# Two fused transformer layers on one core: the first weight pairs' sums moved into the preamble, and block 1's rotary scores moved behind two projection steps

## The chip, the cores and the metric

The kernel runs on one core of a Trainium2 chip. The metric is device time in microseconds of one execution, the median of several runs. Names of engines: TensorE (PE) does matmuls and writes PSUM; VectorE (DVE) and ScalarE (ACT) work element by element on SBUF and PSUM; GpSimd (POOL) works on SBUF; SP issues most of the DMA transfers.

## The reference, cut to what matters

Four batches of 256 tokens, 256 features, go through two layers with a layer norm after each half:

```python
x = layernorm(x + L0_attn(x));  x = layernorm(x + L0_ffn(x))
x = layernorm(x + L1_attn(x));  x = layernorm(x + L1_ffn(x))

# L0_attn: 16 heads, plain part 128 wide, rotary part 64 wide
q_rope, k_rope = apply_rope(q_rope, cos, sin), apply_rope(k_rope, cos, sin)
scores = einsum('bqhd,bkhd->bhqk', q_nope, k_nope) / sqrt(128) \
       + einsum('bqhd,bkhd->bhqk', q_rope, k_rope) / sqrt(64)
out = einsum('bhqk,bkhd->bqhd', softmax(scores), v) @ Wo.T
```

`L0_ffn` is a gated network with a Walsh-Hadamard transform of its hidden row, `L1_attn` an mLSTM block with a gated network of its own, `L1_ffn` a gated network with int8 weights. All arithmetic is float32.

## The kernel before

**Attention.** The 16 heads make eight pairs (`NPAIR`), the tokens two halves of 512 (two batches each). A *block* h is one pair p = h // 2 and one half n = h % 2, so there are 16 blocks. Each block's scores, softmax and weighted values (`fast_block`) run together with the projections of the next block (`fast_projections(h + 1)`), whose matmuls fill TensorE while the softmax runs on the other engines. Block 0's own projections are made plainly, in a preamble (`projections(0)`).

**Seven products for eight.** From block 1 on, a projection is a 2 x 2 product of blocks (two column halves of the weights c, two batches b, two halves of the features i), made with seven block products instead of eight. They need sums and differences of the inputs (`input_sums(n)`: four instructions, kept in `xsum`) and of the weights (`weight_sums(p)`, kept in `wsums[p % 2]`: four combinations, each as one instruction for the three plain groups q, k, v, 384 columns, and one for the rotary group, 128 columns: eight in all). `weight_sums(0)` stands in the preamble, `weight_sums(1)` in front of block 1, `weight_sums(p)` in front of block 2p - 2 for the others. Each stands behind the last projection step of the block before, by `behind(...)`, which orders an instruction behind another of its own engine and adds no wait between engines.

**Steps.** The projection products are cut into steps A1 to A7 (groups "rotary" and "q", in the PSUM banks `mm`) and B1 to B7 (groups "k" and "v", in the banks `sc`, or `ot` while block 0 runs). A step is two to four matmuls (on the chip each is two passes) and the copies (ScalarE) or additions (VectorE) that take its results out. Lists fix the order of the steps: `EARLY[0]` and `EARLY[1]` for blocks 0 and 1, `ORDER` for the others; V and O are the weighted values and the output product of the block before. `EARLY[1]` begins `A1 A2 B1 B2 A6 A7 B6 B7`. A7 accumulates on a bank whose content A2's additions (`qn`, line 375) must first have read.

**Rotary part.** When A3 and A4 are done, `turn(0)` and `turn(1)` swap neighbouring rows (a shuffle on VectorE, line 291) and multiply and add on GpSimd, three instructions each (lines 294 to 296); the last writes `kr`. In `projections(0)` the same is done at lines 183 to 188. `turned_weights` copies the rotary columns of a pair into another order on GpSimd (line 115).

**Scores.** `scores` issues 16 matmul passes per score bank group for the plain part (line 434), then those of the rotary part (line 445), which need `kr`. A score bank is one of two `sc` or two `pt` banks; it is read by `maxima` (line 456, VectorE) and by two exponentials (line 465, ScalarE).

**Order of loads.** SP's queue takes the loads in program order: pair 0's weights in pieces, the tables, the second half of `xT`, `w_o` of pair 0, the residual rows `acc` (two loads of 0.5 MB, line 136), pair 1's weights (1 MB) and `w_o`, then three 1-MB weights of the first feed-forward network. All of `acc` is first used when the output product of block 0 is added to it (line 547).

**Later stages.** `ffn0(n)`, `mlstm(n)`, `ffn1(n)` are generators; each `yield` carries an amount of time. `merge(first, other)` runs `first` and, for every amount it yields, takes steps of `other` until their amounts (1.7 for most) cover it, so that `other`'s matmuls fill TensorE while `first` waits for the other engines. `mlstm_in` yields 9.0 after a norm, in front of the transposes of its result `hin`; `chain(take(1, one), [6.0])` runs the norm at the start of `ffn1(0)` and covers it with 6.0 of ffn0(1). A scheduler then fixes the order on each engine.

Of the kernel before, what the change touches and what calls it, by code (L numbers as in the profile page):

```python
# [39 lines left out]
def tile_two_layers(ctx: ExitStack, tc: tile.TileContext, a: dict, out: bass.AP):  # L40
# [90 lines left out]
    had = cst[:, 512:640]  # L131
    mask = cst[:, 640:768]
    ident = cst[:, 896:1024]
    acc = [wts.tile([P, NJH, D], F32, tag=f"acc{n}", name=f"acc{n}") for n in range(2)]
    for n in range(2):
        nc.sync.dma_start(acc[n], a["x"][:, n * NJH : (n + 1) * NJH, :])
    weights[1], w_os[1] = load_pair(1), load_output(1)

    def ff_weight(name, engine=nc.sync, dtype=F32):

# [15 lines left out]
    rotated = {}  # L156
    QB, XB = P // 32, S // 32

    nothing = lambda: None

    def projections(h):


        p, n = divmod(h, 2)
        w, wr = weights[p]
        qn = attn.tile([P, 2, HALF], F32, tag="qn", name="qn")
        kn = attn.tile([P, 2, HALF], F32, tag="kn", name="kn")
        qr = attn.tile([P, HALF], F32, tag="qr", name="qr")
        kr = attn.tile([P, HALF], F32, tag="kr", name="kr")
        v = attn.tile([P, NJH, 2 * P], F32, tag="v", name="v", bufs=3)  # L170

        def product(wcols):
            ps = bank("mm")
            mm_k(ps, wcols, lambda i: xT[:, i, n * HALF : (n + 1) * HALF], KC)
            return ps

        def rope(k, scale, dst):

            ps = product(lambda i: wr[:, i, k, :])
            raw = attn.tile([P, HALF], F32, tag="raw", name="rope_raw", bufs=3)  # L180
            nc.scalar.mul(raw, ps, scale)
            swp = attn.tile([P, HALF], F32, tag="swp", name="rope_swp", bufs=3)
            nc.vector.stream_shuffle(swp, raw, SWAP)
            by_b = lambda t: t.rearrange("p (b s) -> p b s", s=S)
            cs, sn = (t.unsqueeze(1).to_broadcast([P, 2, S]) for t in (cos, sin))
            nc.gpsimd.tensor_tensor(by_b(raw), by_b(raw), cs, ALU.mult)
            nc.gpsimd.tensor_tensor(by_b(swp), by_b(swp), sn, ALU.mult)
            rotated[h] = nc.gpsimd.tensor_tensor(dst, raw, swp, ALU.add)

        def nope_q2():  # L190

            ps = [bank("mm") for _ in range(2)]
            for i in range(KC):
                for e in range(2):
                    nc.tensor.matmul(
                        ps[e], lhsT=w[:, i, e * P : (e + 1) * P], rhs=xT[:, i, n * HALF : (n + 1) * HALF],
                        start=(i == 0), stop=(i == KC - 1),
                    )
            for e in range(2):
                nc.scalar.mul(qn[:, e, :], ps[e], QSCALE)  # L200

        def nope_q(e):
            ps = product(lambda i: w[:, i, e * P : (e + 1) * P])
            return nc.scalar.mul(qn[:, e, :], ps, QSCALE)

        def nope_k(e):
            ps = product(lambda i: w[:, i, 384 + e * P : 384 + (e + 1) * P])
            return nc.scalar.copy(kn[:, e, :], ps)

        def values(jj):  # L210
            ps = bank("mm")
            for t in range(2):
                j = n * NJH + 2 * jj + t
                mm_k(
                    ps[:, t * 256 : (t + 1) * 256],
                    lambda i: xT[:, i, j * P : (j + 1) * P],
                    lambda i: w[:, i, 768:1024],
                    KC,
                )
            return nc.vector.tensor_copy(  # L220
                v[:, 2 * jj : 2 * jj + 2, :], ps.rearrange("p (t d) -> p t d", t=2)
            )

        units = [lambda: rope(0, RSCALE, qr), lambda: rope(1, 1.0, kr)]
        units += [lambda e=e: nope_q(e) for e in range(2)] if h else [nope_q2, nothing]
        units += [lambda e=e: nope_k(e) for e in range(2)]
        units += [lambda jj=jj: values(jj) for jj in range(2)]
        return (qn, kn, qr, kr, v), units
# [22 lines left out]
        nc.vector.tensor_tensor(three, xT[:, 1, tok(1)], xT[:, 0, tok(1)], ALU.subtract)  # L251
        return nc.vector.tensor_tensor(four, xT[:, 1, tok(0)], two, ALU.subtract)

    def weight_sums(p):

        w, wr = weights[p]
        sums = wsums[p % 2]
        plain = lambda i, c: w[:, i, :].rearrange("p (g c x) -> p g c x", g=3, c=3)[:, :, c, :]
        rot = lambda i, c: wr[:, i, c, :]
        for at, three in (  # L260
            (lambda m: sums[:, m, 0:384].rearrange("p (g x) -> p g x", g=3), plain),
            (lambda m: sums[:, m, 384:512], rot),
        ):
            nc.vector.tensor_tensor(at(0), three(0, 1), three(1, 1), ALU.add)
            nc.vector.tensor_tensor(at(1), at(0), three(0, 0), ALU.subtract)
            nc.vector.tensor_tensor(at(2), three(0, 0), three(0, 1), ALU.subtract)
            last = nc.vector.tensor_tensor(at(3), three(1, 0), at(1), ALU.subtract)
        return last

    def fast_projections(h):  # L270
# [16 lines left out]
        def turn(c):  # L287

            swp = attn.tile([P, HALF], F32, tag="swp", name="rope_swp", bufs=3)
            with tc.issue_after(settled["softmax"].ins):  # L290
                nc.vector.stream_shuffle(swp, raw[c], SWAP)  # L291
            by_b = lambda t: t.rearrange("p (b s) -> p b s", s=S)
            cs, sn = (t.unsqueeze(1).to_broadcast([P, 2, S]) for t in (cos, sin))
            nc.gpsimd.tensor_tensor(by_b(raw[c]), by_b(raw[c]), cs, ALU.mult)  # L294
            nc.gpsimd.tensor_tensor(by_b(swp), by_b(swp), sn, ALU.mult)  # L295
            rotated[h] = nc.gpsimd.tensor_tensor((qr, kr)[c], raw[c], swp, ALU.add)
# [121 lines left out]
        steps.update({"B" + k: f for k, f in pair_of_groups("sc" if h > 1 else "ot", (1, 2)).items()})  # L418
        return (qn, kn, qr, kr, v), steps

    def scores(t, batches):

# [5 lines left out]
        for bb in batches:  # L430
            for e in range(2):
                for qt in range(2):
                    in_turn(
                        lambda: nc.tensor.matmul(  # L434
                            ps[bb][e][:, qt * S : (qt + 1) * S],
                            lhsT=qn[:, e, queries(bb, qt)], rhs=kn[:, e, keys(bb)],
                            start=(qt == 0), stop=False, skip_group_check=True,
                        )
                    )
        for bb in batches:  # L440
            for qt in range(2):
                for e in range(2):
                    rows = slice(e * DR, (e + 1) * DR)
                    in_turn(
                        lambda: nc.tensor.matmul(  # L445
                            ps[bb][e][:, qt * S : (qt + 1) * S],
                            lhsT=qr[rows, queries(bb, qt)], rhs=kr[rows, keys(bb)],
                            start=False, stop=(qt == 1), skip_group_check=True,
                        )
                    )  # L450
# [98 lines left out]
        steps = halves()  # L549
        return lambda: next(steps, None)  # L550

    settled = {}
    behind = lambda ins: tc.issue_after(ins.ins)

    ORDER = "A1 A2 V00 A6 V01 A7 A5 B1 B2 A3 A4 B6 B7 V10 B5 V11 O0 B3 O0 B4 O1 O1".split()
    EARLY = {
        0: "A1 A2 B1 A6 B2 A7 A5 B6 A3 B7 B5 A4 B3 B4".split(),
# [1 line left out]
    }  # L559
    def fast_block(h, t, probs, prev, steps):  # L560

        ps = scores(t, (0, 1))
        crossed = crossing()
        po, outs, last = {}, {}, {}
        top = [maxima(ps[bb][e]) for bb in range(2) for e in range(2)]
        found = [exponentials(ps[0][0], top[0])]

# [5 lines left out]
        for step in EARLY.get(h, ORDER):  # L573
# [6 lines left out]
                    outs[bb] = output_product(h - 1, bb, po[bb])  # L580
            elif step[0] == "O":
                settled["block"] = outs[int(step[1])]()
            else:
                settled["block"] = last[step] = steps[step]()
            if step == "A1":
                with behind(last["A1"]):
                    found.append(exponentials(ps[0][1], top[1]))
# [17 lines left out]
    tiles, units = projections(0)  # L605
    settled["inputs"] = input_sums(0)
    with behind(settled["inputs"]):
        for u in units[2:4] + units[0:2]:
            u()
        settled["weights"] = weight_sums(0)  # L610
    for u in units[4:6]:
        u()
    with behind(settled["weights"]):
        for u in units[6:]:
            settled["values"] = u()
    with behind(settled["values"]):
        input_sums(1)
    with behind(rotated[0]):
        turned_weights(*weights[1])
    after_it, steps = fast_projections(1)  # L620
    probs, prev = None, None
    for h in range(NB - 1):
        for p in range(1, NPAIR):
            if h == max(1, 2 * p - 2):
                with behind(settled["block"]):
                    weight_sums(p)
        probs = fast_block(h, tiles, probs, prev, steps)
        if h % 2 == 0:
            if 0 < h < NB - 2:
# [220 lines left out]
    def mlstm_in(n, t):  # L850

        hin = work.tile([P, NJH, D], F32, tag="hin", name=f"hin{n}")
        rmsnorm(xb[n], hin)
        yield 9.0
        fm = feature_major(n)
        transposed(hin, fm, "m", vecs[:, 0:2])
        yield 1.7
# [371 lines left out]
    def chain(*streams):  # L1229
        for s in streams:  # L1230
            yield from s
# [10 lines left out]
    run(one)  # L1242
    merge(mlstm(0), other)
    one = ffn1(0, "d")
    merge(chain(take(1, one), [6.0]), other)
    run(take(1, one))
    run(other)
    q_gate, q_up, q_down = (ff_weight(k, nc.gpsimd, F32R) for k in ("q_gate", "q_up", "q_down"))
# [123 lines left out]
```

## Time and profile before

| | us |
|---|---|
| median of three runs | 699.29 (698.92 to 705.53) |
| the profiled execution | 699.31 |
| its span, first to last instruction | 697.5 |
| mean granted TensorE clock | 0.995 |
| DMA moved | 45.43 MB, mean 65 GB/s |
| PE busy, 0 to 20 us of the span | 19.22 |
| PE busy, 20 to 40 | 19.59 |
| PE busy, 40 to 60 | 17.41 |
| PE busy, 60 to 80 and 80 to 100 | 20.00 each |
| PE busy, 640 to 697 | 49.95 of 57 |

Durations and starts are those of one profiled execution. A matmul of float32 appears as two passes, and matmuls overlap, so the time that one costs is the distance from start to start. A line of the waits reads: engine, its line, what it waited for, microseconds in all, how often, the longest. A line of the timeline reads: start, length, engine, line of the kernel, operation, what is written and read, shapes, number of instructions merged into the line, and, in brackets, idle time just before it and what ended it.

### The profile page before, as it was taken

The numbers are of one execution on the slowest core, as the hardware profiler recorded it, in microseconds if no ns is written. First come the engines' busy times: TensorE is split into PE (matmuls) and PEld (weight loads), VectorE is DVE, ScalarE is ACT, GpSimd is POOL, SyncE is SP. The second block draws the span as 40 slices with busy tenths as digits, with TensorE's granted clock in tenths as the row PEclk, the third lists the DMA queues.
The fourth block names the chain that finished last, engine by engine and source line by source line (L and its number), as shares of the span: only waits on it lengthen the run. The fifth ranks groups of instructions, "written<-read, shape, count | busy, mean of one in ns | idle before, by whom it ended". The sixth has DMA issues, their size and how long they took to land.

```text
span 697.5 us, 9871 instructions
## 1 busy us (share of the span) xinstructions
PE 685.2 (98%) x3408; PEld 533.0 (76%) x3408; DVE 455.4 (65%) x1238; ACT 260.5 (37%) x773; POOL 178.4 (26%) x187
## 2 busy tenths in 40 slices
PE   9989999999999999999999999999999999999995
PEld 5878888988988898898888764745685558648885
DVE  3996766676577478467547664373878468844767
ACT  2432542443354254334425331037312561111652
POOL 4254314413632740751243100004000130000210
PEclk9999999999999999999999999999999999999999
DMA  8543143232332421521431442003030300000001
GB/s 261 222 122 60 30 109 61 46 95 57 61 97 40 103 65 31 137 56 20 122 62 32 151 96 37 0 1 122 1 121 0 123 2 1 0 0 1 1 0 61
DMA packets 49026, 45.43 MB, mean 65 GB/s; under 512 B 9520, under 2 KB 42704, under 8 KB 47824
## 3 DMA queue, kind: packets, MB, share of 16 engines
q1 hardware_dynamic: 48112, 41.00, 22.8%
q0 software_dynamic: 432, 3.15, 1.3%
q10 hardware_dynamic: 432, 0.66, 0.3%
q8 instruction: 27, 0.44, 0.3%
q14 instruction: 23, 0.19, 0.1%
HBM read 25.61 MB, written 1.08 MB: 38 GB/s over the span
## 4 chain that ended last, share of the span: by engine, by line
PE 89%; DVE 6%; DMA 1%; POOL 1%; ACT 1%; issue 1%; SPq 0%; DVEq 0%; ACTq 0%
PE ps_mm L350 13%; PE ps_d L70 11%; PE ps_m L70 8%; PE ps_ot L70 8%; PE ps_mm L70 8%; PE ps_sc L342 6%; PE ps_sc L350 6%; PE ps_d L797 6%; PE ps_d L1110 4%; PE ps_sc L434 3%; PE ps_pt L434 3%; PE ps_sc L445 2%; PE ps_m L1029 2%; PE ps_m L797 2%; PE ps_pt L445 2%; PE ps_m L766 1%
## 5 line engine op out<-in xcount | busy, mean ns | idle before, releaser
L294 POOL TENSOR_TENSOR rope_raw<-rope_raw,cst 128x512 f32<-128x512 f32 x30 | 38.5, 1285 | 187.3 <-DVE rope_swp L291 187.3
L465 ACT ACTIVATE pr<-ps_sc,nmax 128x256 f32<-128x256 f32 x64 | 29.8, 476 | 128.0 <-DVE nmax L456 128.0
L70 PE MATMUL ps_mm<-w_o,oT 128*128 128x256 f32 x256 | 62.2, 379 | 0.0
L70 PE MATMUL ps_ot<-prT,v 128*128 128x256 f32 x240 | 61.3, 380 | 0.2 <-issue 0.2
L70 PE MATMUL ps_d<-fm,w 128*128 128x512 f32 x128 | 56.8, 595 | 0.0
L547 DVE TENSOR_TENSOR acc<-ps_mm,acc 128x512 f32<-128x512 f32 x32 | 22.1, 691 | 49.8 <-PE ps_mm L70 49.6
L70 PEld LDWEIGHTS ps_mm<-w_o,oT 128*128 128x128 f32 x256 | 46.7, 190 | 5.3
L988 POOL TENSOR_TENSOR ex<-cst,ex 128x512 f32<-128x512 f32 x16 | 19.7, 1263 | 111.9 <-DMA ex<-far 111.9
L70 PEld LDWEIGHTS ps_ot<-prT,v 128*128 128x128 f32 x240 | 43.3, 190 | 5.6 <-issue 0.9
L70 PEld LDWEIGHTS ps_d<-fm,w 128*128 128x128 f32 x128 | 23.9, 190 | 27.2 <-issue 25.4
L350 PE MATMUL ps_mm<-xsum,wsum 128*128 128x256 f32 x180 | 43.9, 380 | 0.4 <-DVE qn L375 0.4
L456 DVE TENSOR_REDUCE nmax<-ps_sc 128x2 f32<-128x512 f32 x32 | 20.6, 686 | 35.7 <-PE ps_sc L445 35.7
L483 DVE STREAM_TRANSPOSE cross<-pr 128x512 f32<-128x512 f32 x60 | 42.7, 711 | 1.5
L364 ACT COPY kn<-ps_sc 128x256 f32<-128x256 f32 x56 | 20.9, 373 | 58.2 <-PE ps_sc L342 58.1
L475 DVE TENSOR_SCALAR pr<-pr,rinv 128x256 f32<-128x256 f32 x128 | 39.4, 349 | 1.8
L295 POOL TENSOR_TENSOR rope_swp<-rope_swp,cst 128x512 f32<-128x512 f32 x30 | 38.5, 1283 | 0.0
L788 ACT ACTIVATE glu_g<-ps_d 128x512 f32<-128x512 f32 x24 | 14.2, 594 | 64.5 <-PE ps_d L70 64.5
L350 PEld LDWEIGHTS ps_mm<-xsum,wsum 128*128 128x128 f32 x180 | 33.9, 190 | 5.0 <-DVE qn L375 0.6
L373 DVE TENSOR_TENSOR kn<-ps_sc,kn 128x256 f32<-128x256 f32 x42 | 17.8, 425 | 28.7 <-ACT kn L364 18.2
L1106 POOL TENSOR_TENSOR qh<-gq,qh 128x512 fp32r<-128x512 f32 x6 | 7.8, 1295 | 96.8 <-issue 85.0
L465 ACT ACTIVATE pr<-ps_pt,nmax 128x256 f32<-128x256 f32 x64 | 30.2, 491 | 2.6 <-DVE nmax L456 2.6
L434 PE MATMUL ps_sc<-kn,qn 128*128 128x256 f32 x128 | 30.2, 379 | 0.0
(271 smaller groups left out, 1571.4 us busy)
## 6 DMA issues: line engine op xcount, KB each, us to landing
prT<-cross SPq DMA_DIRECT2D x240, 64.0 KB, 2.1
w_qkv<-in_w_qkv SPq DMA_DIRECT2D x7, 1024.0 KB, 5.2
ex<-far SPq DMA_DIRECT2D x8, 512.0 KB, 5.6
w<-in_w SPq DMA_DIRECT2D x3, 1024.0 KB, 13.0
w_o<-in_w_o SPq DMA_DIRECT2D x8, 256.0 KB, 2.8
acc<-in_x SPq DMA_DIRECT2D x2, 512.0 KB
w_gate<-in_w_gate SPq DMA_DIRECT2D x1, 1024.0 KB
w_up<-in_w_up SPq DMA_DIRECT2D x1, 1024.0 KB, 4.9
```

Of the source, the lines that this page charges most:

```text
L70: last = nc.tensor.matmul(ps, lhsT=lhs(i), rhs=rhs(i), start=(i == 0), stop=(i == n - 1))
L294: nc.gpsimd.tensor_tensor(by_b(raw[c]), by_b(raw[c]), cs, ALU.mult)
L295: nc.gpsimd.tensor_tensor(by_b(swp), by_b(swp), sn, ALU.mult)
L342: lambda: nc.tensor.matmul(ps[:, k * S + j * P : k * S + (j + 1) * P], lhsT=x[:, j * P : (j + 1) * P], rhs=wt, start=(start and not k and ...
L350: lambda: nc.tensor.matmul(ps[:, k * S : (k + 1) * S], lhsT=wt, rhs=x, start=(start and not k), stop=True, skip_group_check=True,)
L434: lambda: nc.tensor.matmul(ps[bb][e][:, qt * S : (qt + 1) * S], lhsT=qn[:, e, queries(bb, qt)], rhs=kn[:, e, keys(bb)], start=(qt == 0), s ...
L445: lambda: nc.tensor.matmul(ps[bb][e][:, qt * S : (qt + 1) * S], lhsT=qr[rows, queries(bb, qt)], rhs=kr[rows, keys(bb)], start=False, stop= ...
L465: nc.scalar.activation(pr[:, qt, :], ps[:, qt * S : (qt + 1) * S], AF.Exp, bias=nmax[:, qt : qt + 1], accum_out=rsum[:, qt : qt + 1],)
L475: nc.vector.tensor_scalar(pr[:, qt, :], pr[:, qt, :], rinv[:, qt : qt + 1], None, ALU.mult)
L483: return nc.vector.transpose(cross[:, :, e], pr.rearrange("p t (x i) -> p x t i", i=32))
L797: nc.tensor.matmul(po, lhsT=hT[:, i, j * P : (j + 1) * P], rhs=wd[:, i, :], start=(i == 0), stop=(i == NH - 1))
L1110: nc.tensor.matmul(ps, lhsT=lhs, rhs=rhs, start=(k == 0), stop=(k == len(terms) - 1))
```

## The change

It does five things.

1. SP's queue: the load of pair 1's weights and of its `w_o` stands in front of the two loads of `acc`.
2. `weight_sums` takes a list of groups. Pair 0's are made in three parts (rotary; q and k; v), twelve instructions instead of eight, directly behind the first `input_sums` on VectorE, in front of the two shuffles of block 0's rotary part. The second `input_sums` stands behind these shuffles, in front of the value copies. Pair 1's sums (eight instructions, as before) stand behind the value copies, in front of block 0's first maxima, and no longer in front of block 1.
3. In block 1 the steps A1 and A2 are issued between the plain and the rotary scores.
4. In block 0 the shuffles of `turn` are no longer ordered behind the softmax. Their place in VectorE's queue is the same.
5. Two amounts of cover in the later stages: 10.5 instead of 9.0 in `mlstm_in(1)`, and 4.3 instead of 6.0 at the start of `ffn1(0)`.

```diff
+    weights[1], w_os[1] = load_pair(1), load_output(1)
     acc = [wts.tile([P, NJH, D], F32, tag=f"acc{n}", name=f"acc{n}") for n in range(2)]
     for n in range(2):
         nc.sync.dma_start(acc[n], a["x"][:, n * NJH : (n + 1) * NJH, :])
-    weights[1], w_os[1] = load_pair(1), load_output(1)
...
-            nc.vector.stream_shuffle(swp, raw, SWAP)
+            settled["turned"] = nc.vector.stream_shuffle(swp, raw, SWAP)
...
-    def weight_sums(p):
+    def weight_sums(p, groups=((0, 3), (3, 4))):
...
+        for g0, g1 in groups:
+            if g0 == 3:
+                part = lambda i, c: wr[:, i, c, :]
+                at = lambda m: sums[:, m, 384:512]
+            else:
+                part = lambda i, c: w[:, i, :].rearrange("p (g c x) -> p g c x", g=3, c=3)[:, g0:g1, c, :]
+                at = lambda m: sums[:, m, 0:384].rearrange("p (g x) -> p g x", g=3)[:, g0:g1, :]
+            nc.vector.tensor_tensor(at(0), part(0, 1), part(1, 1), ALU.add)
+            nc.vector.tensor_tensor(at(1), at(0), part(0, 0), ALU.subtract)
+            nc.vector.tensor_tensor(at(2), part(0, 0), part(0, 1), ALU.subtract)
+            last = nc.vector.tensor_tensor(at(3), part(1, 0), at(1), ALU.subtract)
         return last
...
-            with tc.issue_after(settled["softmax"].ins):
+            with behind(settled["softmax"]) if h > 1 else contextlib.nullcontext():
                 nc.vector.stream_shuffle(swp, raw[c], SWAP)
...
-    def scores(t, batches):
+    def scores(t, batches, between=lambda: None):
...
+        between()
         for bb in batches:
             for qt in range(2):
...
+        def take_step(name):
+            settled["block"] = last[name] = steps[name]()
...
-        ps = scores(t, (0, 1))
+        ps = scores(t, (0, 1), (lambda: [take_step(k) for k in ("A1", "A2")]) if h == 1 else nothing)
...
     settled["inputs"] = input_sums(0)
     with behind(settled["inputs"]):
-        for u in units[2:4] + units[0:2]:
+        settled["weights"] = weight_sums(0, ((3, 4), (0, 2), (2, 3)))
+    with behind(settled["weights"]):
+        for u in units[2:4] + units[0:2] + units[4:6]:
             u()
-        settled["weights"] = weight_sums(0)
-    for u in units[4:6]:
-        u()
-    with behind(settled["weights"]):
+    with behind(settled["turned"]):
+        settled["inputs"] = input_sums(1)
+    with behind(settled["inputs"]):
         for u in units[6:]:
             settled["values"] = u()
-    with behind(settled["values"]):
-        input_sums(1)
     with behind(rotated[0]):
         turned_weights(*weights[1])
+    with behind(settled["values"]):
+        weight_sums(1)
...
     for h in range(NB - 1):
-        for p in range(1, NPAIR):
-            if h == max(1, 2 * p - 2):
-                with behind(settled["block"]):
-                    weight_sums(p)
+        if h and h % 2 == 0 and h // 2 + 1 < NPAIR:
+            with behind(settled["block"]):
+                weight_sums(h // 2 + 1)
...
-        yield 9.0
+        yield 10.5 if n else 9.0
...
-    merge(chain(take(1, one), [6.0]), other)
+    merge(chain(take(1, one), [4.3]), other)
```

The steps A1 and A2 of block 1 are skipped where the list comes to them again. On TensorE the order changes in three places: the two steps in block 1; ffn1(0)'s transposes, which stand in front of the last four of ffn0(1)'s `down` matmuls instead of behind them; and mlstm(1), where gate and up products of ffn1(0) stand one place further forward, so that three instead of four groups of four `down` matmuls are left between its output product and the transposes of ffn1(1).

## The prediction

> **What bounds the kernel now.** I read the busy times first, then who TensorE (PE) waited for, then the order of time around each of those waits.
>
> ```profile
> PE 685.2 (98%) x3408; PEld 533.0 (76%) x3408; DVE 455.4 (65%) x1238; ACT 260.5 (37%) x773; POOL 178.4 (26%) x187
> ```
>
> PE is busy 685.2 of 697.5 us. A change that removes no PE instruction can win only the gaps in PE's stream. The second view lists them: engine, line, awaited result, total us, times, longest.
>
> ```profile
> PE ps_sc L445 <- POOL kr L296: 2.6, 1, 2.6
> PE ps_pt L82 <- PEq L1361: 0.8, 1, 0.8
> PE ps_mm L350 <- DVE qn L375: 0.4, 1, 0.4
> PE ps_d L70 <- DVE fm L773: 0.4, 1, 0.4
> PE ps_m L766 <- DVE hin L757: 0.3, 1, 0.3
> ```
>
> Four gaps lie where the change works: block 1's rotary scores (2.6), step A7 of block 0 (0.4), the first gate product of ffn1(0) (0.4), the transposes of `hin` in mlstm(1) (0.3). As a matmul's tail is drawn after its slot has passed, the slots lost are a little longer: 256-column matmuls follow each other every 0.2158 us (8 in 1.73), so a gap is measured here from start to start.
>
> The order of time in the preamble (start, length, engine, line):
>
> ```profile
> 13.49 1.37 DVE L264 TENSOR_TENSOR wsum<-w_qkv 128x384 f32<-128x384 f32 x1
> ...
> 19.16 1.67 POOL L188 TENSOR_TENSOR kr<-rope_raw,rope_swp 128x512 f32<-128x512 f32 x1
> ...
> 24.20 1.28 DVE L456 TENSOR_REDUCE nmax<-ps_sc 128x2 f32<-128x512 f32 x2
> ```
>
> Pair 0's sums run beside the rotary work of GpSimd (POOL), and each takes as long as the POOL instruction in front of it; pair 2's in block 2, with POOL idle, do not:
>
> ```profile
> 67.46 0.28 DVE L264 TENSOR_TENSOR wsum<-w_rot 128x128 f32<-128x128 f32 x1
> 67.66 0.55 DVE L267 TENSOR_TENSOR wsum<-w_qkv,wsum 128x384 f32<-128x384 f32 x1
> ```
>
> So 0.55 alone against 1.37, and one starts every 0.47 (384 columns) or 0.20 (128) alone, but every 1.54 or 1.28 beside POOL, whose instruction goes from 1.27 to 1.58. Block 1:
>
> ```profile
> 37.64 1.89 PE L434 MATMUL ps_sc<-kn,qn 128*128 128x256 f32 x8
> ...
> 42.34 1.45 POOL L296 TENSOR_TENSOR kr<-rope_raw,rope_swp 128x512 f32<-128x512 f32 x1
> ...
> 43.85 1.13 PE L445 MATMUL ps_sc<-kr,qr 64*128 64x256 f32 x8 [2.59 <-POOL kr L296]
> ...
> 49.63 1.89 PE L350 MATMUL ps_mm<-xsum,wsum 128*128 128x256 f32 x8
> ```
>
> PE has done its sixteen plain score passes by 37.64 + 3.45 = 41.09 and waits until 43.85 for `kr`. Step A6 starts at 49.63, 11.99 after the first score.
>
> **Block 1: A1 and A2 in front of the rotary scores, pair 1's sums gone from here.** Call the start of the scores N. A1 and A2 are 8 passes, 1.73: PE is done with them at N + 5.18. POOL's chain started at N - 2.31 and has six products; the first three took 3.86 without the sums, so six take 7.7, and `kr` comes at N + 5.42 instead of N + 6.16. PE waits 0.25 to 0.3, not 2.76. The scores end at N + 7.40 (1.93, as before). Next is B1, whose PSUM bank is freed only by the exponentials of the first score bank. That chain is now late: the first maxima start at N + 6.63 (before: 0.19 after the bank's last score), take 0.64 and allow two exponentials at N + 7.36 that take 0.93; B1 starts at N + 8.4, a PE wait of 1.0. B2 needs the second bank, 0.97 later: N + 9.4. A6 follows at N + 10.27, against N + 11.99: 1.72 won. Behind it I find no new wait: ScalarE copies B1 by N + 10.9, B6 wants it at N + 12.0; VectorE adds B2's values by N + 12.65, B7 wants them at N + 12.87, the thinnest cover here. Bounds: 2.8 won if B1 and B2 do not wait, 0.9 if ScalarE's order holds A6 as long again. I take 1.72, the sum of the rows.
>
> **Preamble: where the sums go.** VectorE idles 4.52 in front of 11.16. Pair 0's sums fill that: the rotary part from 7.3, when POOL has copied it; four 128-column sums at 0.20, four of 256 at 0.33 (a start every 0.33 for the 256-column `xsum`), four of 128 at 0.20 give 2.9, without POOL beside them. The last four wait for the value columns, issued at 6.29; loads of this size land after 3.8 (median), so 10.1, and the sums end near 10.9, just ahead of the first shuffle (11.16). These shuffles are now queued behind them, and POOL's rotary chain behind the shuffles: a landing after 5.2, the slowest `w_qkv` load shown, makes the shuffle 1.1 late.
>
> The split makes twelve instructions of eight. [...] The rows give each extra instruction 0.20 + 0.33 - 0.47 = 0.06, 0.24 in all, since the next one starts before the last has ended. [...]
>
> The second `input_sums` moves from 22.74, where POOL was idle, into POOL's chain: four instructions, each behind one POOL product: the two engines alternate from 14.46 and end near 19.5, `kr` at 20.8 as before (20.83). PE wants it at 22.37. Then the value copies, 1.20, to 20.75. Then pair 1's eight sums, new in front of the first maxima: three of 384 columns beside POOL's four copies of 0.32 (3 x 0.42 + 4 x 0.32, to 23.3), then, behind those copies, 0.28 + 0.47 + 3 x 0.20 = 1.35: the maxima start at 24.65 instead of 24.28. I call this 0.37 late. Queued behind it is all VectorE work of block 0; A7 waits for its end (`qn`), had no slack, and passes the 0.37 on to N. Bounds: 0.58 early (A7's whole gap from 28.84 to 29.42 gone, if the sums run in front of POOL's copies and the copies end sooner) to 1.5 late (the late landing above carried through `kr` and the copies).
>
> Pair 1's load passes two 0.5-MB row loads in SP's queue: at the 420 GB/s shown from 14 to 26 it lands 2.4 earlier and the rows some 3 later. Their first use is the addition at 63.72. Before, POOL's copy at 20.77 did not wait for the load, so its cover grows; without it the sums would hold the maxima. No shuffle waits for the softmax any more in block 0, but in VectorE's queue it stands where it stood: nothing. Other blocks keep their order.
>
> **Later stages.** 4.3 for 6.0 moves ffn1(0)'s transposes in front of the last four `down` matmuls (8 passes, 1.73), which then stand between them and the gate product.
>
> ```profile
> 526.21 1.04 PE L766 MATMUL ps_d<-cst,h 128*128 128x128 f32 x8
> ...
> 527.65 1.98 PE L70 MATMUL ps_d<-fm,w_gate 128*128 128x512 f32 x4 [0.41 <-DVE fm L773]
> ```
>
> From 527.08 (eight transposes take 0.87, as from 601.17 to 602.04) to 527.65 is 0.57 lost; the eviction (1.41) now lies under 1.73. The transposes come at 524.48; the last `h` is done at 522.95 + 1.14 = 524.09, so 0.4 is left. I take the 0.57 as won (bounds 0 and 0.6). `hin` needs the last `down`, now 0.87 later on PE, but VectorE gets to it sooner: 0.1 won of 0.47. 10.5 for 9.0 moves whole gate and up steps in mlstm(1) one place forward, and at its end three, not four, `down` groups cover the norm ahead of ffn1(1)'s transposes: 5.18 of matmuls against 4.8 (594.26 to 599.07) plus one addition and statistics that now stand inside (up to 0.8). Transposes start with the first of four `h` parts, so 0.1 lost (0 to 0.4).
>
> **Sum.** 1.72 - 0.37 + 0.57 + 0.1 - 0.1 = 1.92 won. The profiled execution took 699.31, 1.81 of it outside the span; the median is 699.29. So 697.4.
>
> **Rivals.** *Slower: the preamble pays it all back.* Mechanism: pair 0's value sums wait for their load and hold shuffles, POOL's chain, the w_rot copies and the maxima. The other items win 2.29, so it decides once the maxima start after 24.28 + 2.29 = 26.6, `kr` after 22.7, the value load landing after 12.4, 6.1 after its issue. For it: the two `w_o` loads of the same size took 6.2 in the median. Against: they are later in the queue, and `w_qkv` took 5.2 at most. A landing 6.9 after issue gives 700.1. *The covers fail:* block 1 wins 0.9 only, as B1 and B2 wait longer for banks, and the later transposes cost 0.4: 699.31 - 0.9 + 0.37 - 0.57 + 0.3 = 698.5. For it: B7's cover is 0.2. *More is won:* the sums do not delay the maxima (0.58 won instead of 0.37 lost), B1 and B2 wait less (2.3): 699.31 - 0.58 - 2.3 - 0.6 = 695.8.
>
> One thing no edit addresses: the granted clock was 0.75 from 566 to 570 and 0.82 to 574, 4 x 0.25 + 4 x 0.18 = 1.7 us, in the stretch that mlstm(1) reorders. It can go or double.
>
> **How the numbers follow.** Forecast 0.60 (own range 696.6 to 698.3), covers fail 0.17, slower 0.11, more won 0.12. The range 695.3 to 699.5 takes in the three on the winning side and most of the clock's 1.7; the slower case and extremes of the clock are left out. A measurement here can tell about 1%, 7 us. All PE gaps that the change touches sum to some 4.4, so faster by over 1% is nearly excluded (0.02); slower needs a new wait of 9 us, for which I see no mechanism (0.04); within 1% has 0.94.
>
> **What would show it.** Right: PE's wait for `kr` under 0.5 and new short waits in front of B1 and B2; A6 some 10.3 after the block's first score; the maxima of block 0 at 24.3 to 25.2; the gate product of ffn1(0) without a wait. Wrong: first shuffle after 12, a PE wait for `kr` in block 0, A7's gap above 2, or a new PE wait for `h`.

## The result, and the profile after

| us | before | after |
|---|---|---|
| median | 699.33 (15 runs, 698.16 to 705.53) | 697.11 (15 runs, 694.18 to 699.90) |
| profiled execution, its span | 699.31, 697.5 | 697.11, 695.3 |
| mean granted TensorE clock in it | 0.995 | 0.992 |

The ratio of the times is 0.9943 (95% interval 0.9922 to 0.9964): 2.2 us less, within 1%. The busy times, then the whole list of PE's waits in the changed kernel (engine, its line, what it waited for, us, times, longest); its lines stand four to seven further down than before's:

```profile
PE 685.8 (99%) x3408; PEld 533.6 (77%) x3408; DVE 451.3 (65%) x1242; ACT 260.3 (37%) x773; POOL 177.4 (26%) x187
```

```profile
PE ps_sc L354 <- ACT pr L470: 1.0, 1, 1.0
PE ps_pt L82 <- PEq L1368: 0.8, 1, 0.8
PE ps_ot L70 <- issue: 0.2, 1, 0.2
```

None of the four waits that the prediction set out from is left in the list. (From start to start 0.20 of the wait for `kr` remains, 42.03 to 42.23; PE's drawn tail hides it.) One new wait has come: the one in front of B1, for the score bank. The order of time, for the preamble, A7, block 1 and the start of ffn1(0) and mlstm(1):

```profile
10.92 0.72 DVE L185 STREAM_SHUFFLE rope_swp<-rope_raw 128x512 f32<-128x512 f32 x1
...
18.52 1.33 POOL L190 TENSOR_TENSOR kr<-rope_raw,rope_swp 128x512 f32<-128x512 f32 x1
18.65 1.27 DVE L222 COPY v<-ps_mm 128x512 f32<-128x512 f32 x2
...
22.23 1.14 PE L450 MATMUL ps_sc<-kr,qr 64*128 64x256 f32 x8
...
23.00 0.28 DVE L271 TENSOR_TENSOR wsum<-w_rot,wsum 128x128 f32<-128x128 f32 x1
23.39 1.29 DVE L461 TENSOR_REDUCE nmax<-ps_sc 128x2 f32<-128x512 f32 x2
...
28.63 1.56 PE L354 MATMUL ps_mm<-xsum,wsum 128*128 128x256 f32 x6
...
36.85 1.89 PE L438 MATMUL ps_sc<-kn,qn 128*128 128x256 f32 x8
...
40.91 1.26 POOL L300 TENSOR_TENSOR kr<-rope_raw,rope_swp 128x512 f32<-128x512 f32 x1
42.23 1.13 PE L450 MATMUL ps_sc<-kr,qr 64*128 64x256 f32 x8
45.19 0.70 PE L354 MATMUL ps_sc<-xT,w_qkv 128*128 128x256 f32 x2 [0.96 <-ACT pr L470]
...
47.09 1.89 PE L354 MATMUL ps_mm<-xsum,wsum 128*128 128x256 f32 x8
...
524.18 1.41 DVE L780 TENSOR_SCALAR fm<-ps_d,vecs 128x512 f32<-128x512 f32 x2
524.42 1.89 PE L804 MATMUL ps_d<-w,hT 128*128 128x256 f32 x8
526.15 1.88 PE L70 MATMUL ps_d<-fm,w_gate 128*128 128x512 f32 x4
526.85 0.42 DVE L810 SCALAR_TENSOR_TENSOR acc<-ps_d,acc 128x256 f32<-128x256 f32 x1
527.30 0.43 DVE L741 BATCH_NORM_STATS2 ln_st<-acc 128x6 f32<-128x256 f32 x1
...
538.16 1.04 PE L773 MATMUL ps_m<-cst,hin 128*128 128x128 f32 x8
```

Before, in the same places (A7; `fm`, then the statistics of `hin`; the transposes of `hin`; both lines of A7 are cut off by the end of their window, only their starts are read):

```profile
29.42 1.35 PE L350 MATMUL ps_mm<-xsum,wsum 128*128 128x256 f32 x5 [0.41 <-DVE qn L375]
...
526.85 1.41 DVE L773 TENSOR_SCALAR fm<-ps_d,vecs 128x512 f32<-128x512 f32 x2
...
529.51 0.42 DVE L734 BATCH_NORM_STATS2 ln_st<-acc 128x6 f32<-128x256 f32 x1
...
540.24 1.23 PE L766 MATMUL ps_m<-cst,hin 128*128 128x128 f32 x8 [0.31 <-DVE hin L757]
```

Block 1's first score is at 36.85 and step A6 at 47.09, 10.24 later (before: 11.99). `kr` ends at 42.17 and the rotary scores start at 42.23. The first maxima are at 23.39, 0.8 earlier than before (0.24 of that is an earlier first load) although VectorE does pair 1's sums in front of them. The gate product and `hin`'s transposes follow the work in front of them without a gap.

From start to start along PE's stream: 0.24 us come from an earlier first load (PE's first product at 4.77 instead of 5.01, nothing that the change does), 0.55 from A7, 1.75 from block 1, 0.67 around `fm` (0.57 of gap, and 0.10 in the first gate step), 0.66 at `hin`. That is 3.9 us, and the span fell by only 2.2. The rest went into the clock. Slices of 4 us, the first four of the changed kernel, the last of before; the last figures are granted clock, DMA share and GB/s:

```profile
488.00:492.00 4.00, 4.00 (x35) 3.72 (x33) 3.02 (x6) 1.59 (x5) 0.00 (x0) 1.00 0.02 4
492.00:496.00 4.00, 4.00 (x22) 1.73 (x25) 2.13 (x6) 1.13 (x3) 0.00 (x0) 0.57 0.00 0
...
564.00:568.00 4.00, 4.00 (x32) 3.57 (x32) 1.61 (x4) 1.76 (x7) 0.00 (x0) 0.94 0.01 4
568.00:572.00 4.00, 4.00 (x37) 1.79 (x35) 1.71 (x5) 1.34 (x3) 0.00 (x0) 0.63 0.00 0
```

```profile
568.00:572.00 4.00, 4.00 (x25) 1.47 (x28) 1.93 (x5) 1.13 (x3) 0.00 (x0) 0.57 0.02 4
```

The second dip is the one of before; the first is new. In slices of 0.1 us they read 0.50 from 492.45 to 495.86 and from 567.54 to 570.95 (before: 568.02 to 571.43), 3.41 us each, so 1.7 us lost by each: 3.9 less 1.7 is the 2.2.

### The profile page after: what moved, and what is told of

It reads as the page before. It is cut to its first block, busy times and chain, and to the rows that moved or that the text cites. A ratio compares the mean times of both kernels' runs of the same rounds, so it can differ in the third digit from the quotient of the medians.

```text
span 695.3 us, 9871 instructions
## 1 busy us (share of the span) xinstructions
PE 685.8 (99%) x3408; PEld 533.6 (77%) x3408; DVE 451.3 (65%) x1242; ACT 260.3 (37%) x773; POOL 177.4 (26%) x187
## 4 chain that ended last, share of the span: by engine, by line
PE 97%; DVE 2%; ACT 1%; issue 0%; DVEq 0%; ACTq 0%
PE ps_mm L354 13%; PE ps_d L70 12%; PE ps_mm L70 9%; PE ps_m L70 8%; PE ps_ot L70 8%; PE ps_sc L346 6%; PE ps_sc L354 6%; PE ps_d L804 6%; PE ps_sc L438 4%; PE ps_pt L438 4%; PE ps_d L1117 4%; PE ps_sc L450 2%; PE ps_m L1036 2%; PE ps_m L804 2%; PE ps_pt L450 2%; PE ps_m L773 1%
## 6 DMA issues: line engine op xcount, KB each, us to landing
w<-in_w SPq DMA_DIRECT2D x3, 1024.0 KB, 12.4
```

## The experiments

**What block 1's 1.75 us is made of.** Three kernels took the two causes apart: `kr` made sooner, since pair 1's sums no longer alternate with GpSimd there (GpSimd's last three products take 1.59, 1.58 and 1.45 beside them, 1.26, 1.27 and 1.26 in the changed kernel), and the steps put in front of its use.

e1, the changed kernel without the steps:

```diff
-        ps = scores(t, (0, 1), (lambda: [take_step(k) for k in ("A1", "A2")]) if h == 1 else nothing)
+        ps = scores(t, (0, 1), nothing)
```

> The changed kernel with A1 and A2 of block 1 back behind the rotary scores; pair 1's sums stay in the preamble. N is the start of block 1's first score. Theory (block 1's win has two parts, kr made earlier because VectorE's sums no longer stand between GpSimd's products, and the steps that cover what is left of the wait): kr comes at about N + 5.3, TensorE is free at N + 3.45, so a wait for kr of 1.8 to 1.9 comes back, but B1 no longer waits for its score bank, as A1 and A2 stand in front of it: step A6 at N + 10.8 instead of N + 10.24, 0.6 us lost in the profile. Rival (the steps alone carry the 1.75): A6 back at N + 12.0, 1.75 us lost.

e2, the kernel before with the steps alone:

```diff
-        ps = scores(t, (0, 1))
+        ps = scores(t, (0, 1), (lambda: [take_step(k) for k in ("A1", "A2")]) if h == 1 else (lambda: None))
...
-            else:
-                settled["block"] = last[step] = steps[step]()
+            elif step not in last:
+                take_step(step)
```

> The kernel before with nothing but A1 and A2 of block 1 in front of the rotary scores; pair 1's sums stay in front of block 1. Theory: kr still comes at N + 6.16, TensorE is free at N + 5.18, so a wait for kr of 1.0 stays and the wait for the score bank in front of B1 (about 1.0) comes behind it; A6 at N + 11.0 instead of N + 11.99, 1.0 us won. Rival (steps alone): A6 at N + 10.3, 1.7 won.

e6, the changed kernel with pair 1's sums back in front of block 1:

```diff
-    with behind(settled["values"]):
-        weight_sums(1)
...
+        for p in range(1, NPAIR):
+            if h == max(1, 2 * p - 2):
+                with behind(settled["block"]):
+                    weight_sums(p)
```

> The changed kernel with pair 1's sums back in front of block 1, so that the preamble has only pair 0's sums and the second input sums in front of the first maxima. Theory (the first maxima at 23.39 are held by TensorE's scores, not by pair 1's sums): the maxima stay within 0.1 of 23.4 and N within 0.1 of 36.85; in block 1 the wait for kr comes back with 0.9, B1's bank wait is then 1.5, A6 at N + 11.65, 1.4 us lost. By the prediction as it stood (pair 1's sums end last and hold the maxima): the maxima would start 0.5 us or more earlier.

The order of time in e1, e2 and e6, in this order:

```profile
42.16 1.14 PE L450 MATMUL ps_sc<-kr,qr 64*128 64x256 f32 x8 [1.75 <-POOL kr L300]
...
47.94 1.89 PE L354 MATMUL ps_mm<-xsum,wsum 128*128 128x256 f32 x8
```

```profile
44.84 1.14 PE L446 MATMUL ps_sc<-kr,qr 64*128 64x256 f32 x8 [0.87 <-POOL kr L296]
...
48.38 0.70 PE L350 MATMUL ps_sc<-xT,w_qkv 128*128 128x256 f32 x2 [1.54 <-ACT pr L466]
...
50.27 1.89 PE L350 MATMUL ps_mm<-xsum,wsum 128*128 128x256 f32 x8
```

```profile
22.03 1.13 PE L450 MATMUL ps_sc<-kr,qr 64*128 64x256 f32 x8
...
23.19 1.29 DVE L461 TENSOR_REDUCE nmax<-ps_sc 128x2 f32<-128x512 f32 x2 [3.47 <-PE ps_sc L450]
...
46.40 0.70 PE L354 MATMUL ps_sc<-xT,w_qkv 128*128 128x256 f32 x2 [1.54 <-ACT pr L470]
```

| kernel | pair 1's sums | steps first | N | A6 after N | won |
|---|---|---|---|---|---|
| before | block 1 | no | 37.64 | 11.99 | 0 |
| e2 | block 1 | yes | 38.62 | 11.65 | 0.34 |
| e6 | block 1 | yes | 36.65 | 11.64 | 0.35 |
| e1 | preamble | no | 36.79 | 11.15 | 0.84 |
| after | preamble | yes | 36.85 | 10.24 | 1.75 |

I had expected e1's A6 at N + 10.8. (N itself is 0.98 later in e2 than in before, ahead of anything that its edit touches: PE's first product comes 0.17 later and its first eight take 4.34 instead of 3.52.) Neither part carries the 1.75. The steps alone turn 2.59 of waiting for `kr` into 0.87 for `kr` and 1.54 for the bank behind it; the sums alone leave 1.75 for `kr`. For the steps alone I had expected 1.0, because I left out that a later `kr` makes the score bank later too. e6 also answers for the preamble: without pair 1's sums VectorE idles 3.47 us and the maxima still start 1.16 after the rotary scores, as in the changed kernel (22.23 to 23.39). The sums cost nothing there, but they only just fit: in the changed kernel they end at 23.28, 0.11 before the maxima. The medians (e1 697.68, e2 701.55, e6 697.06 against 699.66 to 699.85 for before) do not rank these kernels, since the clock's dips differ between them by more than the steps do. At one clock, 0.997, they stand in the table's order: before 698.2 to 698.6, e2 697.51 and 697.62, e1 695.95 and 696.03, the changed kernel 694.2 to 694.7. (e1 and the changed kernel have the other parts of the change as well.)

**The preamble.** e9 makes pair 1's sums three times, e10 restores the order of the loads, e11 makes pair 0's sums in two parts.

```diff
-        weight_sums(1)
+        settled["again"] = weight_sums(1)
+    with behind(settled["again"]):
+        settled["again"] = weight_sums(1)
+    with behind(settled["again"]):
+        weight_sums(1)
```

> The changed kernel with pair 1's eight sums made three times in the preamble (same result), 16 instructions more on VectorE in front of the first maxima, with GpSimd idle: 8 x 0.47 + 8 x 0.20 = 5.4 us. It sets the price of the slower rival (late maxima). The sums now end at 23.28 and the maxima start at 23.39. Theory (VectorE's work of block 0 has no slack in front of A7, as the prediction says, so each us that the maxima are late holds block 1 by one us): maxima at 28.7, N 5.3 us later, time + 5.3. Rival (block 0 has slack that takes part of it): N less than 4 us later. By either, the point from which late sums cost is a maxima start of 23.4.

```diff
-    weights[1], w_os[1] = load_pair(1), load_output(1)
     acc = [wts.tile([P, NJH, D], F32, tag=f"acc{n}", name=f"acc{n}") for n in range(2)]
...
+    weights[1], w_os[1] = load_pair(1), load_output(1)
```

> The changed kernel with the two loads of acc again in front of pair 1's weights in SP's queue. The traffic of the changed kernel adds up to pair 1's last byte by about 15.2 us; 2.4 us more make 17.6, and the first use, GpSimd's copy of the rotary columns, comes at 19.8. Theory: no wait, maxima at 23.4, N unchanged, 0 us: this part of the change is worth nothing by itself. Rival: the load lands after 19.8 and the copies and the maxima shift by the difference.

```diff
-        settled["weights"] = weight_sums(0, ((3, 4), (0, 2), (2, 3)))
+        settled["weights"] = weight_sums(0, ((3, 4), (0, 3)))
```

> The changed kernel with pair 0's sums in two parts (rotary; q, k and v), 8 instructions instead of 12. [...] But the part of 384 columns now waits as a whole for the value columns. Theory: sums end at 10.5 to 10.9 as before, first shuffle within 0.3 of 10.92, nothing later moves: 0 us. Rival: the wait for the value columns makes the shuffle 0.5 to 1 us late, and the second input sums, value copies and pair 1's sums with it.

The order of time in e9, e10 and e11:

```profile
29.29 1.28 DVE L461 TENSOR_REDUCE nmax<-ps_sc 128x2 f32<-128x512 f32 x2
...
33.08 3.68 PE L354 MATMUL ps_mm<-xsum,wsum 128*128 128x256 f32 x8 [3.57 <-DVE qn L379]
```

```profile
20.96 2.08 POOL L115 COPY w_rot<-w_qkv 128x128 f32<-128x128 f32 x4
```

```profile
9.62 0.56 DVE L268 TENSOR_TENSOR wsum<-w_qkv 128x384 f32<-128x384 f32 x1 [1.50 <-DMA w_qkv<-in_w_qkv]
...
24.18 1.28 DVE L461 TENSOR_REDUCE nmax<-ps_sc 128x2 f32<-128x512 f32 x2
...
29.41 1.99 PE L354 MATMUL ps_mm<-xsum,wsum 128*128 128x256 f32 x8 [0.63 <-DVE qn L379]
```

e9's maxima are 5.5 later than in the changed kernel, its first load (0.41 later) taken off (another 0.33 of this and of N comes from PE's first eight products, 3.85 instead of 3.52); N is at 43.75, 6.5 later. That is not one to one. A7 is 4.0 later only, since it comes 3.79 behind the first maxima and not 5.24: block 0 takes up 1.45 of so long a delay. The clock then adds 1.7 (it went to 0.50 for 3.4 us from 33.1 on, behind PE's 3.57 us of idling), and a new wait for `v` in front of the last B step most of the rest. The medians, 702.43 against 697.11, are 5.3 apart, as expected, but partly by luck: the profiled e9 has that dip in block 0 and one later, where the changed kernel's has two later ones. Without the clock, N is 4.8 later for sums that are 5.5 late. e10's copy of pair 1's rotary columns starts right behind `kr` (20.96), with no wait for the load, and the maxima 1.16 after the rotary scores: the order of the loads won nothing here. That rests on one execution, in which PE's first eight products came 0.40 later and took 0.77 longer, so that the load had 1.16 us more than in the changed kernel (copy at 19.80); where exactly it landed is not shown. e11 began at the same moment as the changed kernel (4.78) and falsifies my expectation. The 384 columns as one part wait 1.50 us for the value columns, the shuffle is at 11.71 instead of 10.92, and 0.79 of it arrives at the maxima (24.18) and 0.78 at N (37.63). So a small delay does pass on to N in full. The third part, four instructions more, saves 0.78 us (one execution).

**Later stages.** e3 is the kernel before with the two amounts alone:

```diff
-        yield 9.0
+        yield 10.5 if n else 9.0
...
-    merge(chain(take(1, one), [6.0]), other)
+    merge(chain(take(1, one), [4.3]), other)
```

> The kernel before with nothing but the two amounts 10.5 and 4.3. Theory from the two traces: the waits for fm (0.57 from start to start) and for hin (0.47) both go, 1.04 us in the profile, all in front of 540 us. By the prediction as it stood: 0.57 won there, 0.1 of hin, 0.1 lost in front of ffn1(1). The granted clock between 470 and 580 may dip at other places than in the kernel before, each dip 1.7 us.

In e3 both gaps are gone and no other wait has come; in front of ffn1(1) 0.06 is lost (the transposes of `h` take 0.93 from start to start instead of 0.87). Of its 12 executions, 9 lie between 697.94 and 698.82 at a clock of 0.994; most of before's are at 0.995, around 699.6. That is some 1.3 us, as the starts say (0.67 and 0.66). e12 is the changed kernel with 9.0 again:

```diff
-        yield 10.5 if n else 9.0
+        yield 9.0
```

> The changed kernel with 9.0 instead of 10.5 in mlstm_in(1); 4.3 stays. hin's transposes then stand half a gate step (0.86 us) further forward and have half a step instead of a whole one between them and the gate products. Theory (the 4.3 brought hin early, as the additions, fm and xs stand in front of its statistics; the 10.5 only has to cover fm): no wait for hin above 0.2, a wait for fm of 0.4 to 0.7 in front of the gate products (line 870), four groups of down in front of the transposes of ffn1(1): + 0.5 us. Rival (the 10.5 is what hin needed): a wait for hin of 0.4 or more, + 1 us.

The order of time in e12:

```profile
537.09 1.52 PE L773 MATMUL ps_m<-cst,hin 128*128 128x128 f32 x8
538.45 1.02 PE L70 MATMUL ps_d<-fm,w_gate 128*128 128x512 f32 x2
539.40 1.07 PE L870 MATMUL ps_m<-fm,w_if 128*32 128x256 f32 x16
```

The transposes of `hin` take 1.52 instead of 1.04, as they run into `hin`'s later parts, and the gate products start 0.58 later than their work explains. My expected wait for `fm` did not appear; the loss is `hin`'s, about half of what the rival had by the starts. The one execution at 0.997 took 695.44, 0.8 to 1.3 more than the changed kernel's 694.2 to 694.7, so the rival's 1 us is not excluded. So 4.3 removes both waits, and 10.5 keeps `hin` clear of a new one of 0.58.

**The clock.** e4 put half of the cover between the two halves of mlstm's short passes (128x33); e7 made these passes twice; e8 halved them, with 66 columns for two heads, so that every second head uses its neighbour's weights and the result is not the reference's.

```diff
-            yield 3.4
             for half in range(2):
+                yield 1.7
                 attend(t, bb, half, hv)
```

> The changed kernel with the cover of 3.4 in front of mlstm's 32 short passes (128x33) cut into two covers of 1.7, one in front of each half of them, so that no run of short passes is longer than 1.9 us. Theory (a dip of the granted clock follows a run of short passes of 3.65 us, in some executions): no slice of 4 us between 470 and 580 under 0.95, every timed execution near the fastest of the changed kernel (694.2 to 694.7, mean clock 0.997), median 694.5, if no new wait for ex arises (up to 0.3 each, four places). Rival (the dips have nothing to do with the short passes): dips stay, times spread over 694, 697 and 700 as before, median 697.

```diff
-        for c in range(2):
+        for c in (0, 1, 0, 1):
             for x in range(HG):
                 nc.tensor.matmul(
```

> The changed kernel with each of mlstm's short passes (128x33) made twice: four unbroken runs of 64 short passes, 7.3 us, where there were 32 in 3.65 us; same result. More work: 4 x 3.65 = 14.6 us. Theory (the granted clock is halved for one window of 3.41 us when the window before it, on a grid of 3.41 us that runs free of the kernel, holds mostly short passes): every run now holds at least one whole window, most runs two, so dips follow every run in every execution, 4 to 8 of them at 1.7 us: fastest executions 694.4 + 14.6 + 6.8 = 716 or more, none at 709, mean clock at most 0.988 in every execution. Rival (the dips come by chance or by power and have nothing to do with the runs): some executions without a dip, near 694.4 + 14.6 = 709.0 at 0.997.

```diff
-            for x in range(HG):
+            for x in range(0, HG, 2):
...
-                    ph[:, (c * HG + x) * DV : (c * HG + x + 1) * DV],
+                    ph[:, (c * HG + x) * DV : (c * HG + x + 2) * DV],
```

> The changed kernel with half as many short passes: one matmul of 66 columns for two heads where there were two of 33 (every second head then uses its neighbour's weights, so part of mlstm's values are not the reference's), four runs of 16 passes, about 2 us each. Theory: no window of 3.41 us can lie inside a run any more, so no execution has a dip between 470 and 580: all at the fastest clock, 0.997, spread under 1 us, time 694.4 - 4 x 1.7 = 687.6. Rival: spread over some 3 us or more as before, part of the executions at 0.992.

Slices of e7, then of e8, then the order of time in e4:

```profile
492.00:496.00 4.00, 4.00 (x30) 4.00 (x29) 0.29 (x1) 0.27 (x1) 0.00 (x0) 0.78 0.01 4
496.00:500.00 4.00, 4.00 (x15) 3.23 (x15) 0.72 (x3) 0.50 (x2) 0.00 (x0) 0.50 0.00 0
500.00:504.00 4.00, 4.00 (x38) 2.00 (x37) 2.84 (x9) 0.63 (x1) 0.00 (x0) 0.87 0.00 0
```

```profile
488.00:492.00 4.00, 3.88 (x22) 2.76 (x21) 3.80 (x8) 2.58 (x9) 0.00 (x0) 1.00 0.00 0
492.00:496.00 4.00, 4.00 (x40) 2.15 (x39) 3.53 (x13) 0.70 (x3) 0.00 (x0) 1.00 0.01 4
```

```profile
488.19 2.55 PE L1036 MATMUL ps_m<-va,ex 128*128 128x33 f32 x16 [0.87 <-DVE ex L1027]
```

e7 had a dip in each of its four runs, which then lasted beyond it, three of 6.8 us (from 494.2, 511.3 and 583.0 on) and one, from 596.6 on, of some 14, an estimate from the mean clock: 0.973 over 723.7 us is 19.5 us lost, the three make 10.2 of it, and the end of the kernel took 2.5 in the changed kernel. All executions lay between 724.22 and 728.77, none near 709, the clock at 0.969 to 0.975. That is more than I expected, since a dip lengthens the very run behind or in which the next one comes (the first run is drawn 9.26 us long, where 7.3 was expected): 694.4 + 14.6 + ten windows at 1.7 = 726. e8 had none: all four executions at 0.997, 689.69 to 690.82. The changed kernel's spread over 5.7 us has become 1.1. The times are not at 687.6: from start to start the four runs became 6.0 shorter (2.09, 2.07, 1.73 and 2.09 instead of 3.49 each), not 4 x 1.7, 1.1 us of new waits came behind them, and in the profiled execution PE's first product was 0.41 later. e4 failed as a cure: 1.7 us do not cover `ex`, PE waited 2.4 us in three places, two dips still came where idling (0.87 in the row shown) and short passes stand together, and its median is 704.88 (the profiled execution, with two dips, took 701.96). Its expectation of a clock without dips is refuted for runs of 1.9 us with a wait in front; for runs without one, e8 holds.

**A better version.** What the change left in block 1 is the 0.96 in front of B1. e5 fills it:

```diff
-        1: "A1 A2 B1 B2 A6 A7 B6 B7 A5 B5 V00 A3 V01 A4 B3 B4 V10 V11 O0 O0 O1 O1".split(),
+        1: "A1 A2 A6 A7 B1 B2 A5 V00 B6 B7 A3 B5 V01 A4 B3 B4 V10 V11 O0 O0 O1 O1".split(),
```

> The changed kernel with block 1's list begun A1 A2 A6 A7 B1 B2 A5 V00 instead of A1 A2 B1 B2 A6 A7 B6 B7. A6 and A7 need only what A1's copies and A2's additions have freed long before, so they fill TensorE while the exponentials free the score bank that B1 wants. Theory (the 0.96 us wait in front of B1 is all that is left to win in block 1): no wait for pr in front of B1, the block's weighted values and output product 0.96 us earlier, -1.0 us at the same granted clock (fastest executions 693.3 instead of 694.2 to 694.7). Rival (ScalarE's copies of B1, now behind all exponentials, hold B6): a new wait of 0.5 to 1.3 in front of B6, 0 won.

```profile
44.59 1.99 PE L354 MATMUL ps_mm<-xsum,wsum 128*128 128x256 f32 x8
46.43 0.59 PE L354 MATMUL ps_sc<-xT,w_qkv 128*128 128x256 f32 x2
```

N is at 37.28 here (its first product came at 5.18). A6 follows the rotary scores at N + 7.31 and B1 comes at N + 9.15, its bank free: no wait is left in the block. The median is 695.18 (six runs, 692.86 to 695.79), 0.9928 of before (0.9909 to 0.9948), against 0.9943 for the change. At the highest clock, 0.997, its one execution is 692.86, where the change has 694.18 to 694.65 and before 698.19 to 698.55. That is 1.3 to 1.8 less than the change, where the wait explains 0.96; what the rest is, one execution does not show.

## Why the prediction was right, and where it was not

**Block 1** went by its steps: `kr` at N + 5.32 (5.42 predicted), 0.20 of waiting for it (0.25 to 0.3), A6 at N + 10.24 (10.27 predicted), a wait for the bank of 0.96 in front of B1 (1.0), B2 at N + 9.32 (9.4), B7's thin cover held. e1, e2 and e6 show that the sum was right for the right reason: it needs both parts.

**Preamble**: the filling of VectorE's idle 4.52 held, the sums ended at 10.53 and the shuffle started unharmed. The step that failed is "pair 1's eight sums, new in front of the first maxima ... 0.37 late": 0.55 were won instead. This part went as the rival "more is won" had it, not as the forecast. (The 0.37 was also misread: 24.28 is the end of the last input sum, the maxima's row says 24.20, so the working gave 0.45.) Three sizes add up to it. GpSimd beside 256-column sums took 1.45 per product, not the 1.58 seen beside 384 columns. `kr` came at 19.85, not 20.8, the value copies ran beside its last product, and VectorE was free at 19.84, not 20.75 (0.24 of both is the earlier first load). Pair 1's sums took 3.44, not 3.9. They end at 23.28, just as PE's rotary scores give the maxima their bank: PE holds them, not VectorE (e6). That they fit into the 3.47 that VectorE has there (e6) is luck; I had not worked out that span. That A7 had no slack and passes a delay on to N was right for small ones: A7's 0.58 of idling became 0.03, and e11's 0.79 arrives as 0.78; of e9's 5.5 only 4.0 reach A7. The slower rival did not come: it needed value columns that land after 12.4, and their first sum starts at 9.52 without a wait (10.1 predicted). Its mechanism is real, though: in e11 the sums wait for these columns until 9.62, and it is the split that keeps this wait off the shuffle (0.78). I had weighed the split only by its instructions' cost, at 0.24 by the rows; in the changed kernel a 256-column and a 128-column sum start 0.33 and 0.20 apart, in e11 a 384-column one 0.47, so each extra instruction cost the 0.06 of the rows. The split's benefit, three times that price, was not in my sum.

**Loads**: no cost, as predicted, and no gain seen (e10, one execution).

**Later stages**: 0.57 for `fm` measured 0.57, with 0.10 more in the first gate step. The `hin` term, "0.1 won of 0.47", was mis-sized: 0.66 won, the gap and 0.18 in which its transposes had waited for parts. I saw that the last `down` comes 0.87 later. I missed that `fm`'s eviction and the four `xs` additions, 2.8 us that stood behind VectorE's last `down` addition, now stand in front of it, so `hin`'s statistics start right behind that addition. Of the 0.1 lost in front of ffn1(1), 0.06 came.

**The clock**, "can go or double", doubled: the second dip. So the sum came out right by two errors that cancel: 3.6 won by the change's own steps where I had 1.92, and 1.7 lost to a second dip for which I had given a price but no cause; why the changed kernel has two dips so often stays open. The median of 697.11 stands 0.3 from the forecast of 697.4 partly by luck.

## What to carry to other kernels

Where a moved instruction could land beside other work, find out which engine ends last there before its length is counted as a loss: here VectorE had 3.47 us to spare for sums of 3.44, and PE set the time. A wait that is covered by moved steps shows up again at the next resource that the same chain frees (here 2.59 for `kr` went, and 0.96 for the score bank came), so price the pair (result late, bank late) together, and fill the second one with steps that need neither, as e5 does. With effects of 1 to 3 us, compare executions at the same granted clock, and look for the dips in the profile before a difference of medians is put down to an edit.

## What the runs showed of the hardware that I had not expected

PE's clock halves while PE is busy throughout. In the kernels with runs of 32 passes of 33 columns, drawn 3.65 us long, each such dip is 0.50 for 3.41 us and begins in or right behind a run; in the slices in front of the dips of before and of the changed kernel PE counts as busy 4.00 of 4.00 us and its weight loads take 3.57 to 3.76. The dips lie on a grid: in the changed kernel they begin at 492.5 and 567.5, in e2 at 494.9 and 570.0, both 75.1 apart (22 x 3.41 is 75.0), in e4 at 489.8 and 503.5, 13.7 apart (4 x 3.41 is 13.6). Twice the passes gave dips in every execution (e7, clock 0.969 to 0.975), half of them none (e8, 0.997 in all four).

Idling is followed by a dip too: in e9 PE idles from 29.51 to 33.08, and the clock is 0.50 from 33.14 to 36.55. But the dips at 492 and 568 come without any idling. What counts here is how much of a window, 3.41 us from one point of the grid to the next, a run fills: lay the grid of each trace over its runs, and in the five traces whose rows show both (before, the changed kernel, e2, e5, e6) the 7 dips between 480 and 580 us all follow a window that holds 3.1 us or more of a run, and no window with 2.6 or less is followed by one (by the lengths drawn). So by these runs a window full of short passes can be followed by half the clock, as the idle one in e9 is. Whether it is their width or the weight loads in front of them that counts, no run separates.

The grid explains why the time moves in steps of about 1.7 us: it lies differently in each trace (the dip at the third run begins 3.67 us behind that run's start in before, 3.73 in the changed kernel, 3.36 in e2, 3.26 in e5), and with it changes which runs fill a window. Of before's 64 executions measured beside the experiments 40 had a clock of 0.994 to 0.996 (698.8 to 700.4 us), 5 had 0.997 (698.2 to 698.6) and 19 less (701.6 and more); the changed kernel's 15 had 0.997 five times (694.2 to 694.7) and 0.991 or 0.992 eight times (697.0 to 697.7). Why it has two dips more often than before does is not shown. The distance between its runs does not explain it: without a dip between them, the first and the third run start 73.32 apart in before (21.5 windows) and 73.70 in e1 (21.6), which has the changed kernel's later stages. At equal clock, 0.997, the change is worth 3.8 us (medians 694.4 and 698.2), which agrees with the 3.9 of the starts.
